# Three shared-expert products done as seven products of halves, and two routed sums moved ahead of the conditional block

## The chip, the cores and the metric

The kernel runs on one core of one Trainium2 chip. The core has a matrix engine (TensorE, PE in the profile), a vector engine (VectorE, DVE), a scalar engine (ScalarE, ACT), a general engine (GpSimd, POOL) and a queue engine (SyncE, SP). Each executes its own instructions strictly in the order in which they were written and waits on semaphores for the others. 16 DMA engines move data between the chip's large memory (HBM) and the on-chip memory; transfers are issued by SP (plain copies) and POOL (row gathers by a list of indices). TensorE writes into eight PSUM banks of 128 x 512 f32. The metric is the device time of one execution in microseconds (us).

## The reference

One transformer-like block on x of shape (B, T, H) = (4, 512, 512), all in float32. A conditioned layer norm, a time mix and a channel mix with its own residuals come first; then a second conditioned layer norm gives the rows h for a mixture of experts:

```
h = _layernorm(x) * (1 + cb) + sb
sh_mid = gelu(einsum('th,ehd->ted', xt, Wsh_up))            # 2 shared experts, H 512 -> D 256, every row
shared_out = einsum('ted,edh->th', sh_mid, Wsh_down)        # D 256 -> H 512, summed over both experts
probs = softmax(xt @ W_router); top_v, top_i = top_k(probs, 2)
rt_mid = gelu(einsum('th,ehd->ted', xt, Wrt_up))            # 16 routed experts, two of them for each row
routed_out = einsum('ted,edh->th', rt_mid * gate, Wrt_down)
x = x + gb * (shared_out + routed_out)
```

The reference computes all 16 routed experts; the kernel computes only the two that a row has picked.

## The kernel before, in words

**Stages.** Time mix for the batches 0 to 3, then channel mix (whose large products are already done as seven products of half-size blocks instead of eight), then the experts. The times at which they lie in the profile: the experts begin at about 720 us and end with the span.

**Who decides the order.** Nothing is scheduled by a planner: the instruction order on each engine is the order of the Python code. Where two stages are to overlap, one is a generator that is advanced by the other: `weave(main, back, plan)` runs `main` to its next `yield` and then advances `back` by the next number of the plan (1 when the plan has run out). For batch 1 the time mix is woven with `time_front(2)`, the layer norms of batch 2, by the plan (2, 1, 2, 1, 2) (L1376). A step of `time_front` holds a tile's `statistics` (L194 to L199), `nm` (L212), the normed rows `xn_ln` (ACT, L219) or the transposes `ps_t_ln` (PE, L226).

**Buffers.** 64 row tiles of 128 x 512 f32 (`row_tile`, tag "t", used in rotation: a new tile waits for all users of the tile that is given up), 8 weight tiles of 1 MB (`wpool`: two stay with the shared experts `wsh_0` and `wsh_1`, six hold the weights of routed experts), and 8 PSUM banks in two tags ("ps" and "acc") of four each.

**Routed experts: slots.** The rows are sorted by expert into slots of 128 rows. 41 slots (N_FIRST) always run; up to 6 more run under `tc.If(n_used > N_FIRST)` (L1426), which this data does not take. `slots_by(b)` = 23, 31, 39, 47 says after which slot all rows of batch b are done. The loop is a pipeline of five steps over the slots. Iteration s issues: `turn(s)` (four transposes of the gathered rows, L1222, copied by DVE, L1224), `up(s-1)` (L1230, GELU on ACT L1232), `turn_mid(s-2)` (L1238, copied by DVE, L1240), `down(s-3)` (L1246, copied by ACT, L1248), `keep(s-4)` (store of 256 KB to y_d by SP, L1252) and then `fetch(s+3)`: a gather of 128 rows by POOL (L1207) and two loads of 512 KB of weights by SP (L1201, L1202). No weight can be loaded more than three slots ahead, and a load waits until `down` has freed its tile.

**Shared experts.** Per batch, `shared_up` makes four groups of PE work (per expert and half of D: four k-steps of 128 x 512, L1152) with a GELU on ACT each (L1158), and `shared_down` four more (one per tile of 128 rows, four steps of 128 x 512, L1166), which `scaled_onto` multiplies by gb (L1177) and adds to x (L1178) on DVE. `shared_up` of batches 0 and 1 and `shared_down` of batch 0 run before the slots (L1398). Then `groups`, `shared_down(1)` and `shared_up(2)`, is advanced by one group after every other slot: s = 22, 24, 26, 28 and s = 30, 32, 34, 36. The four groups of `shared_up(3)` (`last_ups`) follow in the iterations 41 to 44.

**Routed results.** `gather(b, t)` (POOL, L1276) brings two rows of y_d per token for tile t: for batch 0 at s = 28 to 31, batch 1 at s = 36 to 39, batch 2 at s = 43 and 44 (two tiles each), batch 3 after the conditional block. `routed` (ACT L1292 multiplies one by its gate; DVE L1293 adds the other; then `scaled_onto`) does batches 0 and 1 two iterations after their gather, `store_out` (SP, L1305) one later.

**Tail.** After the conditional block, for the eight tiles of batches 2 and 3: four matmuls of `shared_down` (L1166), then `routed_and` on DVE, which adds both routed rows to the PSUM tile (L1300, L1301) and then calls `scaled_onto`: four DVE operations per tile. The last tile's routed part is done apart (L1293), and its shared part in two halves of 256 columns (L1444) that lie in one PSUM bank, each with a multiply (L1452), an add (L1453) and a store.

## Time and profile before

| | |
|---|---|
| device time, median of 3 runs | 1027.38 us (1027.22 to 1028.17) |
| the profiled execution, its own time | 1028.34 us |
| its span, first to last instruction | 1026.5 us (1.84 us lie around the span) |
| TensorE busy | 1003.0 us, 98%, granted clock 0.997 |
| VectorE, ScalarE, GpSimd busy | 616.8, 319.8, 342.3 us |
| moved by DMA | 182.83 MB |

How to read it: busy times of the engines overlap, so they are not added up; what counts is the chain in which each piece waits for the one before. A matmul's shown duration runs from its issue to its modelled end; the next one starts before that end, so the distance from start to start is what a matmul costs in a dense row. A float32 matmul of the code appears as two records. "DMA share" in a table by stretches is the mean busy share of the 16 DMA engines (it can be a little above 1 by its reckoning), beside the GB/s that they moved.

### The profile page before, as it was taken

What the parts mean: (1) busy time and instruction counts of PE and PEld (TensorE: products, weight loads), DVE (VectorE), ACT (ScalarE), POOL (GpSimd) and SP (SyncE); (2) the same over time, 40 slices, a digit from 0 to 9 for tenths busy, and PEclk for the clock granted to TensorE, in tenths of its full rate; (3) what the DMA queues carried; (4) which work ended last, traced back from release to release, by engine and by line L of the source; (5) the groups of instructions that cost most, each with busy time, mean ns of one, the idle gap of its engine ahead of it and who ended that gap; (6) DMA issues with size and microseconds to landing.
All of it is one profiled execution on the core that took longest, in us unless ns stands there. A gap on an engine that the chain in (4) does not pass through costs nothing. (4 is left out here: it accounts for less than half of the span.)

```text
span 1026.5 us, 11651 instructions
## 1 busy us (share of the span) xinstructions
PE 1003.0 (98%) x3930; PEld 685.8 (67%) x3930; DVE 616.8 (60%) x1181; ACT 319.8 (31%) x530; POOL 342.3 (33%) x324
## 2 busy tenths in 40 slices
PE   7999999999999999999999999999998999999997
PEld 2444444444688888888888888888646676666643
DVE  5787887797665736848757587428654222233426
ACT  1765645653222305320262203220021222122310
POOL 2463563514354105620266006520104221232160
PEclk9999999999999999999999999999999999999999
DMA  9600401352069562365226534650536999899762
GB/s 328 247 0 2 125 19 42 103 192 86 1 225 349 178 233 83 121 232 178 88 76 215 195 133 175 240 180 1 185 123 187 365 382 383 270 321 316 266 194 83
DMA packets 96765, 182.83 MB, mean 178 GB/s; under 512 B 7528, under 2 KB 50280, under 8 KB 92608
## 3 DMA queue, kind: packets, MB, share of 16 engines
q1 hardware_dynamic: 90864, 162.92, 45.6%
q0 software_dynamic: 5840, 19.14, 5.8%
q8 instruction: 32, 0.52, 0.2%
q14 instruction: 29, 0.24, 0.1%
HBM read 149.75 MB, written 32.29 MB: 177 GB/s over the span
## 5 line engine op out<-in xcount | busy, mean ns | idle before, releaser
L199 POOL TENSOR_TENSOR rstd_ln<-rstd_ln,minus_half 128x1 f32<-128x1 f32 x64 | 42.9, 672 | 199.5 <-DVE rstd_ln L198 182.5
L782 PE MATMUL ps_y<-wval,a 128*128 128x256 f32 x384 | 86.0, 380 | 0.0
L1207 POOL DMA_INDIRECT xg<-h_d,token x41 | 39.5, 963 | 127.9 <-PE ps_xt L1222 44.8
L782 PEld LDWEIGHTS ps_y<-wval,a 128*128 128x128 f32 x384 | 72.3, 190 | 12.0 <-issue 2.5
L1230 PE MATMUL ps_up<-wrt,xt 128*128 128x256 f32 x328 | 78.0, 381 | 0.3 <-ACT act L1232 0.2
L1246 PE MATMUL ps_down<-wrt,at 128*128 128x512 f32 x164 | 77.2, 593 | 0.0
L1230 PEld LDWEIGHTS ps_up<-wrt,xt 128*128 128x128 f32 x328 | 59.1, 190 | 8.0 <-DVE xt L1224 1.0
L1224 DVE COPY xt<-ps_xt 128x512 f32<-128x512 f32 x41 | 28.2, 689 | 56.2 <-PE ps_xt L1222 42.1
L711 PE MATMUL ps_ky<-T,keys_hi 128*128 128x256 f32 x256 | 60.6, 380 | 0.0
L711 PE MATMUL ps_kx<-mix_ln,keys_lo 128*128 128x256 f32 x256 | 60.5, 379 | 0.0
L357 PE MATMUL ps_o<-wo,av 128*128 128x512 f32 x128 | 57.4, 597 | 2.4 <-DVE x L427 1.2
L352 PE MATMUL ps_r<-mix_ln,wr 128*128 128x512 f32 x128 | 57.6, 593 | 0.8 <-issue 0.8
L782 PE MATMUL ps_z<-wval,a 128*128 128x256 f32 x256 | 57.9, 380 | 0.0
L352 PE MATMUL ps_v<-mix_ln,wv 128*128 128x512 f32 x128 | 57.5, 592 | 0.0
L782 PE MATMUL ps_x<-wval,a 128*128 128x256 f32 x256 | 57.2, 379 | 0.0
L1152 PE MATMUL ps_up_sh<-h,wsh 128*128 128x512 f32 x128 | 57.2, 593 | 0.0
L394 DVE RECIPROCAL p<-p 128x512 f32<-128x512 f32 x16 | 53.6, 3353 | 0.6
L1166 PE MATMUL ps_down_sh<-wsh,mid 128*128 128x512 f32 x120 | 53.1, 595 | 0.3 <-PEq L1426 0.3
L711 PEld LDWEIGHTS ps_kx<-mix_ln,keys_lo 128*128 128x128 f32 x256 | 48.5, 190 | 6.9 <-issue 0.5
L711 PEld LDWEIGHTS ps_ky<-T,keys_hi 128*128 128x128 f32 x256 | 48.3, 190 | 6.8 <-DVE ku L749 0.4
L782 PEld LDWEIGHTS ps_z<-wval,a 128*128 128x128 f32 x256 | 48.1, 190 | 6.8 <-issue 0.6
L782 PEld LDWEIGHTS ps_x<-wval,a 128*128 128x128 f32 x256 | 48.2, 190 | 6.3
(260 smaller groups left out, 1845.3 us busy)
## 6 DMA issues: line engine op xcount, KB each, us to landing
wrt<-in_rt_up_dram SPq DMA_DIRECT2D x41, 512.0 KB
wrt<-in_rt_down_dram SPq DMA_DIRECT2D x41, 512.0 KB
wval<-sums_d SPq DMA_DIRECT2D x16, 1024.0 KB
wval<-in_wval_t_dram SPq DMA_DIRECT2D x12, 1024.0 KB
keys_lo<-keys_d SPq DMA_DIRECT2D x12, 1024.0 KB
y_d<-y SPq DMA_DIRECT2D x41, 256.0 KB
keys_hi<-keys_d SPq DMA_DIRECT2D x12, 768.0 KB
mod<-mod_d SPq DMA_DIRECT2D x22, 256.0 KB
```

Source lines behind the costliest of these rows:

```text
L199: nc.gpsimd.tensor_tensor(rstd, rstd, minus_half, ALU.pow)
L352: nc.tensor.matmul(ps, w[:, k, m * P : (m + 1) * P], acts[k], start=(k == 0), stop=(k == NK - 1))
L357: nc.tensor.matmul(ps, acts[k][:, t * P : (t + 1) * P], w[:, k, :], start=(k == 0), stop=(k == NK - 1))
L394: nc.vector.reciprocal(p, p)
L711: nc.tensor.matmul(ps[:, c * HT : (c + 1) * HT], w[:, k, c * P : (c + 1) * P], acts[k], start=(fresh and c == 0 and k == 0), stop=(c == 1 ...
L782: nc.tensor.matmul(ps[:, j * HT : (j + 1) * HT], acts[p][:, c, j * P : (j + 1) * P], w[:, i, :], start=(fresh and i == 0 and j == 0), stop ...
L1152: nc.tensor.matmul(ps, wu[:, k, m * P : (m + 1) * P], h3s[b][k], start=(k == 0), stop=(k == NK - 1))
L1166: nc.tensor.matmul(ps, mids[b][j][:, t * P : (t + 1) * P], shared[j // ND][1][:, j % ND, :], start=(j == 0), stop=(j == len(mids[b]) - 1),)
L1207: nc.gpsimd.indirect_dma_start(out=xg, out_offset=None, in_=h3_d, in_offset=bass.IndirectOffsetOnAxis(ap=token[:, s : s + 1], axis=0),)
L1224: nc.vector.tensor_copy(xt.rearrange("p k t -> p (k t)"), ps)
L1230: nc.tensor.matmul(ps[:, :D], xt[:, k, :], wu[:, k, :], start=(k == 0), stop=(k == NK - 1))
L1246: nc.tensor.matmul(ps, at[:, j, :], wd[:, j, :], start=(j == 0), stop=(j == ND - 1))
```

## The change

Three of the eight shared products are done as seven products of half-size blocks (`shared_down(1)`, `shared_up(2)` and `shared_up(3)`); the products of batch 0, `shared_up(1)` and the `shared_down` of batches 2 and 3 stay direct.

- `shared_sums` (new) makes eight sums or differences of weight blocks on DVE (128 x 512 each), in the slot loop at s = 3; one of them overwrites a block of `wsh_1` in place.
- `shared_down_terms` and `shared_up_terms` (new) make the sums of the other operand on DVE, one slot ahead of the group: at s = 23, 28 and 40.
- `seven` (new) issues the seven products (28 matmuls of 256 columns), with the additions that combine them on DVE and three copies by ACT. The groups are no longer spread: `shared_down(1)` lies in one piece after slot iteration 24, `shared_up(2)` after 29, both with a short rest of DVE work an iteration later; of `shared_up(3)` four products are issued at s = 41 and three after the loop.
- `shared_up` now writes its GELU results in pieces of 128 x 256 (two ACT instructions in place of one), since blocks of halves are needed.
- `routed(2, 0)` and `routed(2, 1)` are issued before the rest of `shared_up(3)` and the conditional block, wholly on DVE (the gate's multiply too).
- In the tail `routed_and` is gone. The routed sums are issued one tile ahead (`routed`: ACT, DVE), and `scaled_onto` takes the PSUM tile alone. The two halves of the last tile lie in PSUM banks of their own.
- The weave plan for batch 1's time mix is (2, 2, 1, 2) in place of (2, 1, 2, 1, 2).

The diff, cut to its core:

```diff
     def shared_up(b, halves=False):
-        mids[b] = []
-        for wu, _ in shared:
+        mids[b] = [[row_tile(f"mid_{b}_{t}_{f}", (P, ND, HT)) for f in range(E_SH)] for t in range(2)]
+        for f, (wu, _) in enumerate(shared):
             for m in range(ND):
-                ps = bank(f"ps_up_sh_{b}_{len(mids[b])}")
+                ps = bank(f"ps_up_sh_{b}_{f}_{m}")
                 for k in range(NK):
                     nc.tensor.matmul(
                         ps, wu[:, k, m * P : (m + 1) * P], h3s[b][k], start=(k == 0), stop=(k == NK - 1)
                     )
                     if halves and k % 2:
                         yield
-                act = row_tile(f"mid_{b}_{len(mids[b])}", (P, T))
-                nc.scalar.activation(act, ps, AF.Gelu)
-                mids[b].append(act)
+                for t in range(2):
+                    nc.scalar.activation(mids[b][t][f][:, m, :], ps[:, t * HT : (t + 1) * HT], AF.Gelu)
...
+    def shared_sums():
+        for i, j in blocks:
+            ups[f"A{i + 1}{j + 1}"] = shared[i][0][:, j * ND : (j + 1) * ND, :]
+            downs[f"B{i + 1}{j + 1}"] = shared[i][1][:, :, j * HT : (j + 1) * HT]
+        def add(where, name, one, other, op):
+            where[name] = row_tile(f"sh_{name}", (P, ND, HT))
+            nc.vector.tensor_tensor(where[name], where[one], where[other], op)
+        add(ups, "S3", "A11", "A21", ALU.subtract)
+        ups["S1"] = ups["A21"]
+        nc.vector.tensor_add(ups["S1"], ups["A21"], ups["A22"])
+        add(ups, "S2", "S1", "A11", ALU.subtract)
+        add(ups, "S4", "A12", "S2", ALU.subtract)
+        add(downs, "T1", "B12", "B11", ALU.subtract)
+        add(downs, "T3", "B22", "B12", ALU.subtract)
+        add(downs, "T2", "B22", "T1", ALU.subtract)
+        add(downs, "T4", "B21", "T2", ALU.subtract)
...
+    def seven(name, product, A, Bs, use, parts=False):
+        X = bank(f"{name}_x")
+        product(X, A["A11"], Bs["B11"], True)
+        c1 = copied(f"{name}_c1", X)
+        Y = bank(f"{name}_y", "acc")
+        product(Y, A["S2"], Bs["T2"], True)
+        u = row_tile(f"{name}_u")
+        nc.vector.tensor_add(u, c1, Y)
+        Z = bank(f"{name}_z", "acc")
+        product(Z, A["S1"], Bs["T1"], True)
+        c5 = copied(f"{name}_c5", Z)
+        nc.vector.tensor_add(c5, c5, c1)
+        product(X, A["A12"], Bs["B21"], False)
+        use(0, 0, X)
+        if parts:
+            yield
+        product(Y, A["S3"], Bs["T3"], False)
+        nc.vector.tensor_add(c5, c5, Y)
+        use(1, 1, c5)
+        product(Z, A["S4"], Bs["B22"], False)
+        nc.vector.tensor_add(u, u, Z)
+        use(0, 1, u)
+        product(Y, A["A22"], Bs["T4"], False)
+        yield
+        nc.vector.tensor_add(c1, c1, Y)
+        use(1, 0, c1)
+        yield
+    def halves_product(stationary, moving):
+        def product(ps, a, b, fresh):
+            for c in range(2):
+                for k in range(2):
+                    nc.tensor.matmul(
+                        ps[:, c * HT : (c + 1) * HT],
+                        stationary(a, k, c),
+                        moving(b, k),
+                        start=(fresh and c == 0 and k == 0),
+                        stop=(c == 1 and k == 1),
+                        skip_group_check=True,
+                    )
+        return product
+    acts_of = {}
+    def shared_up_terms(b):
+        acts = {f"B{i + 1}{j + 1}": [h3s[b][2 * i + k][:, j * HT : (j + 1) * HT] for k in range(2)] for i, j in blocks}
+        for name, one, other in (("T1", "B12", "B11"), ("T3", "B22", "B12"), ("T2", "B22", "T1"), ("T4", "B21", "T2")):
+            t = row_tile(f"h3_{name}_{b}", (P, 2, HT))
+            acts[name] = [t[:, k, :] for k in range(2)]
+            for k in range(2):
+                nc.vector.tensor_sub(acts[name][k], acts[one][k], acts[other][k])
+        acts_of[b] = acts
+    def shared_up_seven(b, parts=False):
+        acts = acts_of.pop(b)
+        mids[b] = [[None] * 2 for _ in range(2)]
+        def use(f, t, v):
+            act = row_tile(f"mid_{b}_{t}_{f}")
+            nc.scalar.activation(act, v, AF.Gelu)
+            mids[b][t][f] = act.rearrange("p (c t) -> p c t", c=2)
+        product = halves_product(lambda w, k, c: w[:, k, c * P : (c + 1) * P], lambda a, k: a[k])
+        yield from seven(f"up_sh_{b}", product, ups, acts, use, parts)
...
+    def shared_down_seven(b):
+        A = acts_of.pop(b)
+        def use(i, j, v):
+            at = slice(j * HT, (j + 1) * HT)
+            add = row_tile(f"add_sh_{b}_{i}_{j}", (P, 2, HT))
+            row = gbs[b][:, None, at].broadcast_to([P, 2, HT])
+            nc.vector.tensor_tensor(add, v.rearrange("p (t o) -> p t o", t=2), row, ALU.mult)
+            for t in range(2):
+                xt = x1s[b][2 * i + t][:, at]
+                nc.vector.tensor_add(xt, xt, add[:, t, :])
+        product = halves_product(lambda a, k, c: a[:, k, c * P : (c + 1) * P], lambda w, k: w[:, k, :])
+        yield from seven(f"down_sh_{b}", product, A, downs, use)
...
-    def routed(b, t):
+    def routed(b, t, engine=None):
         g0, g1 = gates_of(b, t)
         y0, y1 = got.pop((b, t))
-        nc.scalar.activation(y1, y1, AF.Copy, scale=g1)
+        if engine is nc.vector:
+            nc.vector.tensor_scalar(y1, y1, g1, None, ALU.mult)
+        else:
+            nc.scalar.activation(y1, y1, AF.Copy, scale=g1)
         nc.vector.scalar_tensor_tensor(y0, y0, g0, y1, ALU.mult, ALU.add)
-        scaled_onto(b, t, y0)
-    def routed_and(b, t, ps):
-        g0, g1 = gates_of(b, t)
-        y0, y1 = got.pop((b, t))
-        nc.vector.scalar_tensor_tensor(y0, y0, g0, ps, ALU.mult, ALU.add)
-        nc.vector.scalar_tensor_tensor(y0, y1, g1, y0, ALU.mult, ALU.add)
         scaled_onto(b, t, y0)
     def store_out(b, t):
...
-        weave(time_mix(b), back, (2, 1, 2, 1, 2) if b == 1 else ())
+        weave(time_mix(b), back, (2, 2, 1, 2) if b == 1 else ())
...
-    groups = chained(lambda: shared_down(1), lambda: shared_up(2))
-    last_ups = shared_up(B - 1)
+    down_1 = slots_by(0) + 1, lambda: shared_down_terms(1), chained(lambda: shared_down_seven(1))
+    up_2 = slots_by(0) + 6, lambda: shared_up_terms(2), chained(lambda: shared_up_seven(2))
+    up_3 = N_FIRST, lambda: shared_up_terms(3), chained(lambda: shared_up_seven(3, True))
     at = [slots_by(b) + 5 for b in range(B - 1)]
     for s in slots(0, N_FIRST, ready):
-        if s >= slots_by(0) - 1 and (s - slots_by(0)) % 2:
-            next(groups, None)
+        if s == AHEAD:
+            shared_sums()
+        for lag, (first, terms, group) in ((-1, down_1), (-1, up_2), (-1, up_3), (0, down_1), (0, up_2), (1, down_1), (1, up_2)):
+            if s == first + lag:
+                if lag < 0:
+                    terms()
+                else:
+                    next(group)
...
-        if s >= N_FIRST:
-            next(last_ups)
-    drain(groups)
-    drain(last_ups)
+        if s == N_FIRST:
+            next(up_3[2])
+    for t in range(NT // 2):
+        routed(B - 2, t, nc.vector)
+    for group in (down_1, up_2, up_3):
+        drain(group[2])
     n_used = nc.values_load(used[0:1, 0:1], min_val=0, max_val=N_SLOT)
     with tc.If(n_used > N_FIRST):
         drain(slots(N_FIRST, N_SLOT))
     for t in range(NT):
         gather(B - 1, t)
-    for b in (B - 2, B - 1):
-        for t in range(NT):
-            ps = down_bank(b, t)
-            if b == B - 1 and t == NT - 1:
-                break
-            down_products(b, t, ps, range(4))
-            if b == B - 1 and t == NT - 2:
-                routed(b, NT - 1)
-            routed_and(b, t, ps)
-            store_out(b, t)
+    rest = [(B - 2, t) for t in range(NT // 2, NT)] + [(B - 1, t) for t in range(NT)]
+    routed(*rest.pop(0))
+    for n in range(2 * NT - 1):
+        b, t = B - 2 + n // NT, n % NT
+        ps = down_bank(b, t)
+        down_products(b, t, ps, range(4))
+        scaled_onto(b, t, ps)
+        store_out(b, t)
+        if rest:
+            routed(*rest.pop(0))
     last = x1s[B - 1][NT - 1]
     for at in (slice(0, HT), slice(HT, H)):
+        ps = bank(f"ps_last_{at.start}", "acc")
         for j in range(4):
             nc.tensor.matmul(
-                ps[:, at],
-                mids[B - 1][j][:, (NT - 1) * P :],
+                ps[:, :HT],
+                mid_of(B - 1, j, NT - 1),
                 shared[j // ND][1][:, j % ND, at],
                 start=(j == 0),
                 stop=(j == 3),
             )
-        add = row_tile(f"add_last_{at.start}")
-        nc.vector.tensor_mul(add[:, at], ps[:, at], gbs[B - 1][:, at])
-        nc.vector.tensor_add(last[:, at], last[:, at], add[:, at])
+        add = row_tile(f"add_last_{at.start}", (P, HT))
+        nc.vector.tensor_mul(add, ps[:, :HT], gbs[B - 1][:, at])
+        nc.vector.tensor_add(last[:, at], last[:, at], add)
         nc.sync.dma_start(out[B - 1, (NT - 1) * P :, at], last[:, at])
```

More of the change, by code (lines that the diff above doesn't have):

```diff
@@ L1162, in shared_up, with mid_of @@
         h3s[b] = None
+    def mid_of(b, j, t):
+        return mids[b][t // 2][j // ND][:, j % ND, (t % 2) * P : (t % 2 + 1) * P]
+    blocks = [(i, j) for i in range(2) for j in range(2)]
+    ups, downs = {}, {}
+    def shared_sums():
[14 more added lines that the diff above has]
+        add(downs, "T4", "B21", "T2", ALU.subtract)
@@ new lines, in copied @@
+    def copied(name, ps):
+        t = row_tile(name)
+        nc.scalar.activation(t, ps, AF.Copy)
+        return t
+    def seven(name, product, A, Bs, use, parts=False):
[25 more added lines that the diff above has]
+        yield
@@ new lines, in shared_up_seven @@
+    def shared_up_seven(b, parts=False):
[7 more added lines that the diff above has]
+        yield from seven(f"up_sh_{b}", product, ups, acts, use, parts)
+        h3s[b] = None
@@ new lines, in shared_down_terms @@
+    def shared_down_terms(b):
+        A = {f"A{t + 1}{f + 1}": mids[b][t][f] for t, f in blocks}
+        for name, one, other, op in (
+            ("S1", "A21", "A22", ALU.add),
+            ("S2", "S1", "A11", ALU.subtract),
+            ("S3", "A11", "A21", ALU.subtract),
+            ("S4", "A12", "S2", ALU.subtract),
+        ):
+            A[name] = row_tile(f"mid_{name}_{b}", (P, 2, HT))
+            nc.vector.tensor_tensor(A[name], A[one], A[other], op)
+        acts_of[b] = A
+    def shared_down_seven(b):
[10 more added lines that the diff above has]
+        yield from seven(f"down_sh_{b}", product, A, downs, use)
@@ L1167, in down_products @@
                 ps,
-                mids[b][j][:, t * P : (t + 1) * P],
+                mid_of(b, j, t),
                 shared[j // ND][1][:, j % ND, :],
                 start=(j == 0),
-                stop=(j == len(mids[b]) - 1),
+                stop=(j == E_SH * ND - 1),
             )
```

## The prediction

> **What bounds the kernel now.** I read the page first, then the table by stretches, then the order of time on TensorE, then the chain of waits at the end.
>
> ```profile
> span 1026.5 us, 11651 instructions
> ...
> PE 1003.0 (98%) x3930; PEld 685.8 (67%) x3930; DVE 616.8 (60%) x1181; ACT 319.8 (31%) x530; POOL 342.3 (33%) x324
> ```
>
> TensorE is the bound: only 23.5 us of the span are not its work, and the list of its waits names 1.8 us of them in time mix and 3.3 us in the tail. So a change is worth what it takes from TensorE's stream, less the waits that it puts in. Inside the slots the stretches say something else as well:
>
> ```profile
> 800.00:810.00 10.00, 10.00 (x46) 6.89 (x45) 2.66 (x5) 2.56 (x5) 2.08 (x3) 1.00 1.06 379
> ...
> 900.00:910.00 10.00, 10.00 (x38) 5.97 (x37) 3.36 (x6) 1.96 (x4) 5.67 (x6) 1.00 0.98 332
> ...
> 920.00:930.00 10.00, 10.00 (x40) 6.31 (x39) 4.52 (x9) 3.39 (x6) 2.02 (x2) 1.00 0.94 297
> ...
> 940.00:950.00 10.00, 10.00 (x40) 6.34 (x39) 2.23 (x4) 2.41 (x5) 5.67 (x6) 1.00 0.95 316
> ```
>
> The columns after each engine's busy time are the clock, DMA share and GB/s. In plain slots (first row) TensorE is full and the DMA engines are full too, 1.06. A plain iteration moves 1.573 MB (two weights of 512 KB, a gather and a store of 256 KB) and takes 4.10 us: 384 GB/s. There DMA has nothing to spare. Only the groups of shared work between the slots give it time.
>
> ```profile
> 878.02 3.60 PE L1166 MATMUL ps_down_sh<-wsh,mid 128*128 128x512 f32 x8
> 881.45 0.60 PE L1222 MATMUL ps_xt<-ident,xg 128*128 128x128 f32 x4
> 881.89 1.89 PE L1230 MATMUL ps_up<-wrt,xt 128*128 128x256 f32 x8
> 883.62 0.38 PE L1238 MATMUL ps_at<-ident,act 128*128 128x128 f32 x2
> ```
>
> From start to start, eight records of 512 columns take 881.45 - 878.02 = 3.43 us, eight of 256 columns 1.73 us. The "mean ns" of the groups (593 and 380) overlap and would mislead.
>
> **The change, part by part.**
>
> *Seven products.* A direct shared product is 4 groups x 8 records of 512 columns: 4 x 3.43 = 13.72 us. Seven products are 28 matmuls, 56 records of 256: 7 x 1.73 = 12.11 us, 1.6 us less. Down 1 and up 2 give -3.2 if nothing waits inside. The additions (128x512 on DVE, 0.69 to 0.75 each) and ACT copies (0.60) stand beside: a bank is written again 3.46 us after its first product, and in one place 1.73 us after, behind one DVE add of 0.72 and at most 1.5 us of `use` begun a product earlier. It is tight but fits; a wait would cost up to 0.8 a group: -3.2, ends -3.2 and -1.6. Their terms (four 128x512 or eight 128x256 adds, 3 us) lie on a DVE that is busy 2.7 to 4.5 of 10 us. The doubled GELUs of batches 0 and 1 (two 128x256 of 0.4 for one of 0.60, every 3.43 us on an ACT at 31%) cost nothing; were that cover gone, 16 x 0.2 = 3.2.
>
> *Weight sums at s = 3.* Eight DVE operations go in behind at_1's copy and ahead of xt_4's.
>
> ```profile
> 788.61 0.41 DVE L1240 COPY at<-ps_at 128x256 f32<-128x256 f32 x1
> 788.94 0.68 DVE L1224 COPY xt<-ps_xt 128x512 f32<-128x512 f32 x1
> ...
> 792.96 1.24 PE L1230 MATMUL ps_up<-wrt,xt 128*128 128x256 f32 x5
> ```
>
> at_1 is done at 789.02; eight adds, start to start 0.72 as L1177's, end at 794.8; xt_4's copy (0.69) at 795.5. The up products that read it began at 792.96, so TensorE waits 2.5 us. at_2's copy, next in the queue, ends at 795.9, before its `down` at 797.4: no second wait. Ends: 2.0 (if an add took 0.66), and 4.2, if the pause also slows the matmuls as the tail's does (1.7, below). Idle times of 1.65 us (786) and 1.81 us (117) were not followed by slow matmuls, one of 3.27 us was; 2.5 is nearer the short ones, so 2.5. The Trainium skill, "TensorE: Matmul & The Clock Gate", Part 1, has the clock halved only after an idle window of about 3.4 us; that adds 0 here (and 1.7 in the other case), though the trace's 3.27 us already was enough.
>
> *Groups taken out of s = 30 to 40.* Before, four groups of up 2 lie there; now eleven plain iterations follow each other, 11 x 4.10 = 45.1 us. They carry 11 x 1.573 = 17.30 MB and, before slot 40's weights, two of batch 0's tiles gathered (1.05), its four stores (1.05) and about half of batch 1's gathers (1.05): 20.45 MB. At 384 GB/s that is 53.3 us. What TensorE's use may lag: a weight is issued at the end of iteration s and first needed in iteration s+4, 12.5 us later; less its slot's own 4.1 us and 2.5 us of latency (batch 2's last gather: issued 984.7, landed 987.3), about 6. 53.3 - 45.1 - 6 = 2.2 us of waiting near s = 38 to 41. Ends: 0 (before, with groups, no wait appears there but 0.8 for rows), and from the mixed rows: at full share 1.06 they would give 332 x 1.06/0.98 = 359, 335 and 353, mean 349 GB/s; 20.45 MB take 58.6 us, a wait of 7.5. I take 2.2, by the full rows, since the mixed ones had moments with nothing issued. SP's and POOL's orders change little otherwise: no transfer passes another on its queue. What speaks against this part in the Trainium skill is "DMA: Bandwidth & Descriptors", Where 436 GB/s comes from: about 358 GB/s bind a core's HBM traffic; then the wait would be 57.1 - 51.1 = 6.0 us and the sum 3.8 worse, but the plain slots ran at 379 to 385.
>
> *Up 3 and the tail.*
>
> ```profile
> 989.98 20.85 PE ps_down_sh L1166 x48
> ...
> 1018.86 0.34 DVE add_last L1452
> 1019.21 0.04 issue
> 1019.25 3.45 PE ps_down_sh L1444 x8
> 1022.72 0.44 DVE add_last L1452
> 1023.18 0.42 DVE x L1453
> ```
>
> The second half of the last tile waits 3.27 us for the multiply that reads the first half from the same bank, and then takes 3.43 in place of 1.73 us. With a bank each, both go: -5.0, and 0.2 of small gaps. Up 3 as seven: -1.6. Against it: the routed sums of batch 2's tiles 0 and 1 (four operations, 2.9 us each) stand on DVE ahead of up 3's last additions. Their gathers landed 11.4 and 13.9 us after up(40) began (968.36), so DVE ends them at about 17.2. The product that waits for the add behind them is due at 17.8, the add takes 0.7: +0.1, and with gathers a little later +0.8, which I take; ends 0 and 2.5 (one gather pair later). In the tail DVE has per tile a multiply and an add from PSUM and a routed sum of three, 5 operations, 3.65 us against 3.43 of TensorE; it has one routed sum less than tiles ahead and none for the last two, falls 1.1 us behind by the fifth and has caught up by the last. ACT's multiply (0.71) fits. Part: -6.0, ends -4.0 and -6.8.
>
> *The weave plan.* Batch 2's tiles 2 and 3 get their statistics a step earlier.
>
> ```profile
> 112.49 3.35 DVE L394 RECIPROCAL p<-p 128x512 f32<-128x512 f32 x1
> ...
> 115.76 0.10 DVE L212 SCALAR_TENSOR_TENSOR nm_ln<-mv_ln,rstd_ln 128x1 f32<-128x1 f32 x1
> ```
>
> nm of tile 3 stands behind the reciprocal, ACT's xn_ln behind nm, and TensorE's transposes wait 1.81 us at 116.77. Now nm precedes the reciprocal: -1.8. Late next is the reciprocal's own chain, 1.2 us (one tile's statistics); its reader has 2.6 us to spare. Ends 0 and -1.8.
>
> **Sum.** -3.2 + 2.5 + 2.2 - 6.0 - 1.8 = -6.3. The profiled execution's 1028.34 us (1026.5 of span, 1.84 around it) would become 1022.0. It lies 0.96 above the median of the three runs; against that median of 1027.38 I get 1021.1, which is my number. 0.2%, about what a measurement of this kernel can tell from no change, is 2.05 us: faster is below 1025.3, slower above 1029.4.
>
> **Rivals.**
>
> *Both new waits are hidden.* DMA keeps its slack (0 for 2.2), the tail gets its best (-6.8): -3.2 + 2.0 - 6.8 - 1.8 = -9.8, 1017.6. For it: DMA had 9 to 11 us of slack between landing and use there before. Against: the groups that gave it are gone.
>
> *DMA is the bound from s = 30 to 41, at a lower rate than the plain slots'.* At 349 GB/s the wait is 7.5 and the sum -1.0: 1026.4, no change. It decides the sign at 10.6 us of waiting: 20.45 MB in 61.7 us, 331 GB/s. At 306, the mean of the rows 920 and 940, it is 66.8 us, a wait of 15.7, +7.2: 1034.6, slower. For it: gathers of rows and writes are mixed with the loads there, and no mixed row but one exceeds 332. Against: TensorE was never held by weights in those rows, and 910 to 920 gave 370.
>
> *The products save nothing.* By the means, seven cost 56 x 380 = 21.3 against 32 x 593 = 19.0 us, +2.3 each, 11.7 us from my sum: +5.4, 1032.8. Against: channel mix runs such products at 1.73 us per eight without a gap.
>
> *DVE sets the tail's end.* 7 x 3.65 = 25.6 against 24.0 and the two waits in it: the part gives -4.0, 1023.1.
>
> **How the numbers follow.** My forecast, with what lies within 3 us of it (the DVE-bound tail too): 0.52. All hidden: 0.14. DMA bound at about 349: 0.12. DMA bound below 331: 0.15. Products without gain: 0.04; the rest 0.03. The range leaves out the two slow cases and little below: from all best (-3.2 + 2.0 + 0 - 6.8 - 1.8 = -9.8, and 1.6 below for what I can't see: 1016) to the end of the 349 case and 1.6 above, 1028. Faster: 0.52 + 0.14 + a part of the 349 case, 0.07: 0.73. Same: 0.05 and the rest, 0.09. Slower: 0.18.
>
> **What would show it.** L226's longest wait for xn_ln at 117 us falls below 0.5. L1230 has one wait of about 2.5 us at 793 for xt. The groups after s = 24 and 29 take 12.1 us without a gap. Between 950 and 965 a wait of TensorE for `wrt` or `xg` of about 2 us in all, and a DMA share above 1 from s = 33 on. No wait at the last halves, both 1.73 us. I am wrong if the waits of s = 30 to 41 pass 5 us, if slow matmuls follow the pause at 793, or if TensorE waits inside `seven`.

## The result, and the profile after

The changed kernel takes 1024.11 us (median of 9 runs, 1022.03 to 1025.98) beside 1027.65 us of the kernel before on the same chip: a ratio of 0.996, 95% interval 0.9947 to 0.9974. It is faster, by 3.5 us where 6.3 were forecast. The profiled execution took 1025.98 us with a span of 1024.3; against the profiled execution of before that is only 2.4 us less, and the readings below account for these two. The nine runs of the changed kernel differ with the granted clock: the three with 0.997 or 0.998 took 1022.03 to 1022.17 us, the six with 0.994 to 0.996, the profiled one among them as the longest, 1023.97 to 1025.98.

The page of the changed kernel begins:

```profile
span 1024.3 us, 11869 instructions
...
PE 1000.3 (98%) x4002; PEld 699.6 (68%) x4002; DVE 646.7 (63%) x1237; ACT 327.0 (32%) x549; POOL 343.8 (34%) x324
```

TensorE is busy 2.7 us less, though three products of 1.6 us each were saved and 1.7 us of slow matmuls at the end are gone: part of its time is spent at a lower clock. Its list of waits (total, times, longest) names what is new:

```profile
PE ps_t_ln L226 <- ACT xn_ln L219: 5.0, 5, 1.5
PE up_sh_y L1233 <- DVE up_sh_c L1216: 2.5, 1, 2.5
...
PE ps_up L1363 <- DVE xt L1357: 1.9, 2, 1.6
PE ps_o L357 <- DVE x L427: 1.7, 3, 1.0
PE ps_down_sh L1299 <- DVEq L1564: 1.1, 1, 1.1
```

The wait of 3.3 us at the last halves is gone, and three others stand in its place: 2.5 us inside up 3, 1.6 us at the slots' end, 1.1 us at the conditional block (L1564). The order of time on TensorE shows where:

```profile
874.07 1.89 PE L1233 MATMUL down_sh_x<-wsh,mid 128*128 128x256 f32 x8
...
884.43 1.89 PE L1233 MATMUL down_sh_y<-sh_T,mid 128*128 128x256 f32 x8
886.16 0.60 PE L1355 MATMUL ps_xt<-ident,xg 128*128 128x128 f32 x4
...
956.50 1.89 PE L1363 MATMUL ps_up<-wrt,xt 128*128 128x256 f32 x8
...
962.34 1.99 PE L1363 MATMUL ps_up<-wrt,xt 128*128 128x256 f32 x8 [1.57 <-DVE xt L1357]
...
966.41 1.97 PE L1363 MATMUL ps_up<-wrt,xt 128*128 128x256 f32 x8
...
982.44 1.89 PE L1233 MATMUL up_sh_z<-h,sh_S 128*128 128x256 f32 x8
986.85 2.55 PE L1233 MATMUL up_sh_y<-h_T,wsh 128*128 128x256 f32 x8 [2.52 <-DVE up_sh_c L1216]
990.46 26.51 PE L1299 MATMUL ps_down_sh<-wsh,mid 128*128 128x512 f32 x56 [1.07 <-DVEq L1564]
1016.81 3.62 PE L1583 MATMUL ps_last<-wsh,mid 128*128 128x256 f32 x16
```

These are the lines of the kernel before for slots 38 and 40 and for the tail:

```profile
960.40 1.89 PE L1230 MATMUL ps_up<-wrt,xt 128*128 128x256 f32 x8
...
968.36 1.99 PE L1230 MATMUL ps_up<-wrt,xt 128*128 128x256 f32 x8
...
989.98 24.27 PE L1166 MATMUL ps_down_sh<-wsh,mid 128*128 128x512 f32 x56 [0.30 <-PEq L1426]
1014.09 1.89 PE L1444 MATMUL ps_down_sh<-wsh,mid 128*128 128x256 f32 x8
1019.25 3.43 PE L1444 MATMUL ps_down_sh<-wsh,mid 128*128 128x256 f32 x8 [3.27 <-DVE add_last L1452]
```

Down 1's seven products take 886.16 - 874.07 = 12.09 us without a gap, and the last halves about 3.5 us together. But the seven tiles of the tail take 1016.81 - 990.46 = 26.35 us, where the kernel before took 24.1 and the kernel without the conditional block, below, 24.04. The stretches (last columns: clock, DMA share, GB/s) say why:

```profile
985.00:990.00 5.00, 2.55 (x8) 1.61 (x8) 2.92 (x5) 1.23 (x2) 0.68 (x2) 0.81 0.45 143
990.00:995.00 5.00, 4.54 (x6) 1.99 (x7) 2.26 (x4) 2.12 (x4) 3.88 (x4) 0.50 0.50 139
995.00:1000.00 5.00, 5.00 (x13) 2.20 (x12) 3.49 (x6) 1.29 (x2) 3.98 (x4) 1.00 0.72 218
```

The granted clock is halved from 988.15 to 994.97: it falls 1.3 us after the pause of 2.52 us, while up 3's last product runs, and is already down when the pause of 1.07 us begins at 989.4. Set against each other, the starts of the same TensorE work in the two profiles, with what the prediction's terms add up to at that point:

| TensorE starts | before | after | difference | predicted |
|---|---|---|---|---|
| k products of batch 2 | 116.93 | 114.80 | -2.13 (-0.38 of it from the first 9 us) | -1.8 |
| o products, batch 2 | 214.25 | 213.55 | -0.70 | -1.8 |
| transposes after channel mix (L923) | 741.32 | 741.24 | -0.08 | -1.8 |
| up(4) | 792.96 | 792.34 | -0.62 | +0.7 |
| up(38) | 960.40 | 956.50 | -3.90 | -2.5 |
| up(40) | 968.36 | 966.41 | -1.95 | -0.3 |
| first matmul of the tail | 989.98 | 990.46 | +0.48 | -1.1 |
| end of VectorE's last addition | 1023.60 | 1021.34 | -2.26 | -6.3 |

At up(40) the changed kernel is 1.6 us ahead of the forecast, by errors of both signs. The forecast was missed behind it: 2.4 us were lost between up(40) and the tail where 0.8 should have been won, and the tail won 2.7 in place of 5.2, because 2.3 went into slow matmuls. Another 0.7 went into up 3's last product, which took 2.55 us in place of 1.89.

### The profile page after: what moved, and what is told of

Same layout as the page of the kernel before. It is cut to its first block, busy times and chain, and to the rows that moved or that the text cites. A ratio compares the mean times of both kernels' runs of the same rounds, so it can differ in the third digit from the quotient of the medians.

```text
span 1024.3 us, 11869 instructions
## 1 busy us (share of the span) xinstructions
PE 1000.3 (98%) x4002; PEld 699.6 (68%) x4002; DVE 646.7 (63%) x1237; ACT 327.0 (32%) x549; POOL 343.8 (34%) x324
## 5 line engine op out<-in xcount | busy, mean ns | idle before, releaser
L1409 POOL DMA_INDIRECT y<-y_d,pos_i x32 | 32.0, 999 | 58.7 <-DMA y_d<-y 35.1
L219 ACT ACTIVATE xn_ln<-x,nm_ln,rstd_ln 128x512 f32<-128x512 f32 x32 | 25.3, 810 | 77.5 <-DVE nm_ln L212 77.5
```

The costliest lines, as they stand in the source:

```text
L1409: nc.gpsimd.indirect_dma_start(out=y, out_offset=None, in_=y_d[: slots_by(b) * P, :], in_offset=bass.IndirectOffsetOnAxis(ap=pos_i[:, c, n ...
```

## The experiments

They ran in three sets, each beside the kernel before on its chip: 1026.36 us in the first (four kernels), 1028.3 and 1028.24 us in the others. Ratios are to these.

### Routed sums behind up 3

```diff
-    for t in range(NT // 2):
-        routed(B - 2, t, nc.vector)
     for group in (down_1, up_2, up_3):
         drain(group[2])
+    for t in range(NT // 2):
+        routed(B - 2, t, nc.vector)
```

> The changed kernel with one edit: the two routed sums of batch 2 stand behind the rest of up 3 on VectorE, not ahead of it (still before the conditional block). Theory 1, the two sums hold up the last product of up 3 and the pause halves TensorE's clock: the wait of 2.52 us at up_sh_y disappears (under 0.5), the clock stays full through the tail, its 56 matmuls of the shared down take 24.0 in place of 26.5 us, and TensorE comes to the last halves 5 to 6 us earlier than in the changed kernel's profile; the end follows if VectorE keeps up, 1019 to 1021 us. Rival, VectorE sets the tail's end: it has the same work left (about 3.65 us per tile and 5.4 us for the two sums), so the end moves by less than 2 us and TensorE waits for banks or VectorE ends alone: 1022 to 1024 us.

Measured: 1026.93 us, 1.0003 (0.9994 to 1.0012), no faster than the kernel before. The wait inside up 3 went, as expected, but TensorE then stood still for longer. TensorE, then VectorE's last routed addition, in order of time:

```profile
984.03 1.89 PE L1233 MATMUL up_sh_y<-h_T,wsh 128*128 128x256 f32 x8
992.26 27.05 PE L1299 MATMUL ps_down_sh<-wsh,mid 128*128 128x512 f32 x56 [6.34 <-DVEq L1564]
...
991.23 0.69 DVE L1311 TENSOR_TENSOR x<-x,add 128x512 f32<-128x512 f32 x1
```

The first tile of the tail needs nothing from the routed sums. It starts 0.34 us after VectorE has left them behind, and the wait is named by VectorE's branch at the conditional block. Both theories had missed this: VectorE does not set the end through its load in the tail, it holds TensorE at the block. A new theory: the PSUM bank of the first tile has its last reader, in program order, inside the block (VectorE's copy `at` of slot 46), and that reader counts as done only when VectorE itself has passed the block, taken or not. The program built from this kernel agrees: the first tile's matmul waits until VectorE's count of finished instructions stands at 1213, which is the copy `at` of slot 46; where the block is not taken, VectorE adds the block's 12 counts in one step, behind a wait for count 1201, its last routed addition.

### The conditional block left out

The kernel of the last experiment without `tc.If`:

```diff
-    n_used = nc.values_load(used[0:1, 0:1], min_val=0, max_val=N_SLOT)
-    with tc.If(n_used > N_FIRST):
-        drain(slots(N_FIRST, N_SLOT))
```

> The kernel with the routed sums behind up 3 (1.0003 of the kernel before), and the conditional block with its six optional slots left out; for these inputs it is not taken, so nothing that is computed is missing. Theory: TensorE's 6.3 us ahead of the tail are a wait for VectorE to pass the block, since the bank of the first tile has its last reader in program order inside it. Without the block the first tile waits for a bank's true last reader: the wait falls to under 1.5 us, the clock stays full, and the end comes 5 to 7 us earlier: 0.993 to 0.996 of the kernel before. Rival, TensorE needs a result of VectorE's queue there (the last addition of up 3 or a routed sum): the wait stays over 3 us and the time within 2 us.

Measured: 1023.95 us, 0.9951 (0.9935 to 0.9967). TensorE goes on without a gap and with the full clock:

```profile
989.42 1.89 PE L1233 MATMUL up_sh_y<-h_T,wsh 128*128 128x256 f32 x8
991.14 24.20 PE L1299 MATMUL ps_down_sh<-wsh,mid 128*128 128x512 f32 x56
```

989.42 + 1.73 = 991.15: no wait at all, with the routed sums in the same place on VectorE, where they end only at 997.3. The block is what ties TensorE to VectorE there. (At 966.28 this profile has a wait of 3.33 us with slow matmuls after it, one of the late signals of the last section.) (In other data, where more than 41 slots are used, this kernel would leave rows out; it is an experiment and not a version.)

### Another bank for the first tile

```diff
-        ps = down_bank(b, t)
+        ps = bank(f"ps_down_sh_{b}_{t}", "ps" if n == 0 else "acc")
```

This too is the kernel with the sums behind up 3.

> The kernel with the routed sums behind up 3 (1.0003 of the kernel before), with one edit: the first tile of the tail lies in a bank of the other tag, whose last user inside the conditional block is read by ScalarE and not by VectorE. Theory: TensorE's 6.34 us ahead of the tail are a wait for VectorE to pass the conditional block, because the bank of the first tile was last read, in program order, by VectorE inside that block. With the other bank the first tile waits for ScalarE alone, which is through at about 987.5: the first tile starts 4 to 5 us earlier (about 987.7) and the second waits at its own bank to about 992.3, so that the tail ends 3.4 us earlier (one tile); with less idle time the halved clock may go as well, 2 us more: -3.4 to -5.5, 0.995 to 0.997. Rival, TensorE waits for the branch value or for VectorE's results: no change, 1.000.

Measured: 1032.46 us, 1.0043 (1.0026 to 1.0059). The wait did not change:

```profile
PE ps_down_sh L1299 <- DVEq L1564: 6.4, 1, 6.4
```

The edit missed its aim: in the program the bank of the other tag, too, is read by VectorE inside the block (the copy `xt` of slot 43), and the first tile waits for that copy beside ScalarE. It tells nothing against the theory and nothing for it. On this chip the kernel also waited 1.86 us at up(39) with slow matmuls after it, which is about the rest of its loss.

### Three products direct again, dense

Down 1, up 2 and up 3 direct in the same places, no sums:

```diff
-        if s == AHEAD:
-            shared_sums()
-    down_1 = slots_by(0) + 1, lambda: shared_down_terms(1), chained(lambda: shared_down_seven(1))
-    up_2 = slots_by(0) + 6, lambda: shared_up_terms(2), chained(lambda: shared_up_seven(2))
-    up_3 = N_FIRST, lambda: shared_up_terms(3), chained(lambda: shared_up_seven(3, True))
+    down_1 = slots_by(0) + 1, lambda: None, chained(lambda: shared_down(1))
+    up_2 = slots_by(0) + 6, lambda: None, chained(lambda: shared_up(2))
+    up_3 = N_FIRST, lambda: None, chained(lambda: shared_up(3))
...
-                if lag < 0:
-                    terms()
-                else:
-                    next(group)
+                if lag == 0:
+                    drain(group)
...
             next(up_3[2])
+            next(up_3[2])
```

> The changed kernel with the three shared products done directly again, in the same places (dense after s = 24, 29, 41 and after the loop), without the sums of weights and of operands; the rest of the change (weave plan, routed sums ahead, new tail) stays. Theory: down 1 and up 2 cost 2 x 1.6 = 3.2 us more, up 3 1.6 more; the wait at s = 3 (0.4) goes, and so does the wait of the last product (2.5), since direct groups wait for no additions, with the halved clock behind it (2.9): net -1.0, 1022 to 1024 us. Rival, the products save nothing by themselves: down 1 takes 12.1 us either way and the result is 3 us or more below the changed kernel. If the halved clock comes without the wait too, the result is above it, 1026.

> All three products direct, dense, with the new tail and plan, as run before (0.9953 of the kernel before): the same again, 0.994 to 0.997, so that the two other kernels of this set are compared with it on one chip.

Measured: 1021.43 us in the first set, 0.9953 (0.994 to 0.9967); 1027.72 us in the third, 0.999 (0.9979 to 1.0). In the first set's profile the tail is what the prediction had drawn:

```profile
980.83 7.03 PE L1153 MATMUL ps_up_sh<-h,wsh 128*128 128x512 f32 x16
988.16 24.27 PE L1299 MATMUL ps_down_sh<-wsh,mid 128*128 128x512 f32 x56 [0.30 <-PEq L1561]
1012.27 3.62 PE L1580 MATMUL ps_last<-wsh,mid 128*128 128x256 f32 x16
```

Direct groups leave VectorE nothing to add, it passes the block early, TensorE waits 0.3 us, and the tail takes 24.1 us. Without any of the seven products the kernel is not slower than the change: on that chip it is the fastest of its set. In the third set the same kernel gained next to nothing; its TensorE waited 1.73 us at 788, 2.17 us at 965 and 1.34 us at 969, none of which the first set's profile has. The last section comes back to that.

### Up 3 alone direct

```diff
-    up_3 = N_FIRST, lambda: shared_up_terms(3), chained(lambda: shared_up_seven(3, True))
+    up_3 = N_FIRST, lambda: None, chained(lambda: shared_up(3))
...
             next(up_3[2])
+            next(up_3[2])
```

Its up 3 reads the block of `wsh_1` that the sums have overwritten, so the shared part of batch 3 is computed from another weight; instructions and sizes are those of the direct product. The kernel of the section after the next shares this.

> The changed kernel with up 3 alone done directly (two groups at s = 41, two after the loop); down 1 and up 2 stay seven products with their sums. Theory: direct groups leave no additions on VectorE behind the routed sums, so VectorE reaches the conditional block before TensorE, TensorE waits 0.3 us there and its clock stays full: 990.46 becomes about 987 and the tail 24.0 us; against the kernel with all three direct (0.9953 of the kernel before) 3.2 us less for the two products, 0.4 more for the sums at s = 3 and 1.7 more for weights that land late at s = 41: -1.1, so about 1020.3 beside 1026.4 of before, 0.994. Rival, the conditional block is not it and the seven products are what costs the time in the slots: no gain over all three direct, 1021.4 or more.

Measured: 1024.34 us, 0.996 (0.9946 to 0.9973). The wait at the block is 0.3 us and the tail 991.00 to 1015.11, 24.1 us, so the block's part of the theory held. The gain over direct products did not show, but the chip was another one, so the comparison was made again side by side:

### Sums one per slot, beside direct products dense and spread

Up 3 direct; the eight sums one per slot from s = 6, S1 in a tile of its own (so nothing is overwritten). The sums' function yields after each, and the loop advances it:

```diff
+    the_sums = shared_sums()
...
-        if s == AHEAD:
-            shared_sums()
+        if s >= AHEAD + 3:
+            next(the_sums, None)
```

> The changed kernel with up 3 direct (down 1 and up 2 stay seven products), the sums of weights one per slot from s = 6 on, in place of eight at s = 3, and none of them in place. Theory: one sum of 0.7 us per slot is hidden, so the two products keep 3.2 us less the 1.7 that late weights take at s = 41: 1.5 us less than the kernel with all three products direct, which runs beside it. Rival, DMA sets the time from s = 30 to 41 and takes all of it: the same time as with direct products, within 0.5 us.

The third kernel has all products direct, and their groups where the kernel before has them:

```diff
+    groups = chained(lambda: shared_down(1), lambda: shared_up(2))
...
+        if s >= slots_by(0) - 1 and (s - slots_by(0)) % 2:
+            next(groups, None)
...
-        if s == N_FIRST:
-            next(up_3[2])
-            next(up_3[2])
+        if s >= N_FIRST:
+            next(up_3[2])
```

> All three products direct, and their groups spread over the slots as in the kernel before (after s = 22, 24, 26, 28; 30, 32, 34, 36; 41 to 44); the new tail and the routed sums ahead of the block stay. Theory: what the change gains is the tail; where the direct groups stand makes no difference, since TensorE waits for no weights in either: within 0.5 us of the dense form beside it. Rival, dense groups cost DMA time that the spread ones use, or the spread ones leave less for the slots at 39 and 40: 1 to 2 us apart.

Measured in one set: seven products with spread sums 1023.89 us, 0.9955 (0.9942 to 0.9968); direct and spread 1024.1 us, 0.9956 (0.9942 to 0.997); direct and dense 1027.72 us. The theory that the place of direct groups makes no difference fell on this chip: dense they were 3.6 us slower, with the waits named above. Two products as seven, dense, worth 3.2 us of TensorE's work, are 3.8 us faster than direct products in the same dense places, but bring nothing over direct groups that are spread. On this chip the late signals of the last section weigh on each of the three differently, so what the seven products are worth by themselves is not settled. TensorE's order of time near the end of the slots shows where their lead goes; first with the seven products:

```profile
956.62 1.89 PE L1370 MATMUL ps_up<-wrt,xt 128*128 128x256 f32 x8
960.00 0.44 PE L1378 MATMUL ps_at<-ident,act 128*128 128x128 f32 x2 [1.49 <-issue]
960.76 3.46 PE L1386 MATMUL ps_down<-wrt,at 128*128 128x512 f32 x4 [0.32 <-DVE at L1380]
...
964.71 1.89 PE L1370 MATMUL ps_up<-wrt,xt 128*128 128x256 f32 x8
...
968.38 1.97 PE L1370 MATMUL ps_up<-wrt,xt 128*128 128x256 f32 x8
```

and then direct and spread, the same three `up` steps (slots 38, 39, 40):

```profile
961.32 1.89 PE L1363 MATMUL ps_up<-wrt,xt 128*128 128x256 f32 x8
...
965.43 1.89 PE L1363 MATMUL ps_up<-wrt,xt 128*128 128x256 f32 x8
...
969.29 1.99 PE L1363 MATMUL ps_up<-wrt,xt 128*128 128x256 f32 x8
```

At up(38) the products have put TensorE 4.7 us ahead, at up(39) 0.7. Here the loss is a late signal with halved clock behind it. On the first set's chip, where no signal was late, the pair of kernels "sums behind up 3" and "direct, dense" gives the same picture by another cause: up(38) at 956.57 against 958.58, 2.0 us ahead, and up(40) at 966.28 against 966.54, 0.3 us. There the list names VectorE's `h_T`, but xt of slot 40 was done at 964.47, and what came last in the trace is slot 40's weights: their last packet landed at 966.14. Whoever comes early waits for them. The changed kernel's own trace agrees: the last recorded packet of these weights landed at 966.28, and its up(40) starts at 966.41, so its wait of 1.57 us at up(39) would have been spent at up(40) otherwise.

### Up 2's products after s = 36

```diff
-    up_2 = slots_by(0) + 6, lambda: shared_up_terms(2), chained(lambda: shared_up_seven(2))
+    up_2 = slots_by(0) + 13, lambda: shared_up_terms(2), chained(lambda: shared_up_seven(2))
```

> The kernel with up 3 alone direct, and up 2's seven products after s = 36 in place of s = 29. Theory: the wait for weights at s = 41 is lack of DMA time between s = 30 and 41; the 12.1 us of products put there give DMA 4.6 MB more time, and the wait of 1.7 us at up(40) goes: 1.7 us less than with the products after s = 29. Rival, the late landing comes from batch 1's gathers at s = 36 to 39 alone, which stay: the wait stays, no difference.

Measured: 1026.88 us, 0.9989 (0.9979 to 0.9999), 2.5 us slower than with the products after s = 29, beside which it ran. At its own place the theory held: up(39) and up(40) follow each other at 967.55 and 971.41, without a wait. But a new wait appears where the products had been:

```profile
903.22 1.89 PE L1363 MATMUL ps_up<-wrt,xt 128*128 128x256 f32 x8
...
913.36 0.44 PE L1371 MATMUL ps_at<-ident,act 128*128 128x128 f32 x2 [4.14 <-issue]
...
912.92 0.38 ACT L1365 ACTIVATE act<-ps_up 128x256 f32<-128x256 f32 x1 [9.34 <-remote]
```

ScalarE's GELU began at 912.92, though the `up` that it reads had been issued at 903.22 and lasted 1.9 us: 7.8 us late. Batch 0's gathers are under way there; with the dense products after s = 29 TensorE has work there that can hide such a delay.

### Sums at s = 10

```diff
-        if s == AHEAD:
+        if s == 10:
             shared_sums()
```

> The changed kernel with the eight sums of weights at s = 10 in place of s = 3. The prediction's step priced them at 2.5 us of waiting of TensorE, and the changed kernel showed 0.5, at a place where TensorE itself was late. Theory: in a settled iteration the price is the full one, one wait of up(11) for xt of 2.3 to 2.7 us at about 820 us, with no slow matmuls after it. Rival, VectorE's queue has room for most of it: under 1 us.

Measured once: 1029.84 us beside 1028.3. The expected wait of 2.3 to 2.7 us does not come; the rival, under 1 us, holds:

```profile
819.45 0.68 DVE L1180 TENSOR_TENSOR sh_S<-wsh,wsh 128x512 f32<-128x512 f32 x1
...
824.83 0.68 DVE L1357 COPY xt<-ps_xt 128x512 f32<-128x512 f32 x1
...
825.56 1.99 PE L1363 MATMUL ps_up<-wrt,xt 128*128 128x256 f32 x8 [0.31 <-DVE xt L1357]
```

Eight sums take 5.4 us, and the `up` was due at 825.1: 0.5 us late. From a settled iteration's `at` copy to the next but one `up` there are 5.6 us and not the 3.9 that the prediction had read at s = 3. The rest of this kernel's loss lies elsewhere: waits of 1.7 us at 788 and 3.25 us at up(39), each with 3.4 us at half clock behind it.

### The weave plan alone

```diff
-        weave(time_mix(b), back, (2, 1, 2, 1, 2) if b == 1 else ())
+        weave(time_mix(b), back, (2, 2, 1, 2) if b == 1 else ())
```

> The kernel before with the new weave plan for batch 1's time mix and nothing else. The prediction's step: -1.8 us, 1025.8 beside 1027.6. Theory now, from the changed kernel's trace: the wait at 117 us goes, but ScalarE and VectorE, which were full there, do not come earlier, so TensorE waits for them at 208 to 214 us and at 739 us, and 0 to -0.4 us are left: 1027.2 to 1027.6.

Measured: 1026.78 us, 1.0003 (0.9994 to 1.0012): nothing. Its TensorE has the three lines that the changed kernel has too:

```profile
116.22 3.60 PE L352 MATMUL ps_k<-mix_ln,wk 128*128 128x512 f32 x8
...
209.76 0.33 PE L226 MATMUL ps_t_ln<-ident,xn_ln 128*128 128x128 f32 x1 [0.38 <-ACT xn_ln L219]
...
214.97 1.55 PE L357 MATMUL ps_o<-wo,av 128*128 128x512 f32 x3 [1.01 <-DVE x L427]
```

Against the run of before's code in the same set (the kernel of the next experiment, which differs from it only in the tail) the transposes at 116 us come 2.12 us earlier and the products at 215 only 0.69, of which 0.38 is an earlier start of the whole sequence in this profile: 1.7 us won and 0.3 left. ScalarE is busy 9.3 and 9.9 of 10 us from 115 to 135 in the kernel before, and its chain with VectorE's reciprocals would then set when the next batches' operands are there; that is argued from these shares and not shown by a run.

### Two banks for the last halves alone

```diff
     for at in (slice(0, HT), slice(HT, H)):
+        ps = bank(f"ps_last_{at.start}", "acc")
         for j in range(4):
```

on the kernel before.

> The kernel before with a PSUM bank of its own for each half of the last tile and nothing else. Theory: the wait of 3.27 us and the slow second half both go, 3.3 + 1.7 = 5.0 us less at most; VectorE's last additions then come 3 us earlier, at the end of its own queue: it is at 1019.2 when the first half's multiply is issued, so the end cannot come before 1018.8 + 4 x 0.43 = 1020.5 us of the span, and I expect -3.0 us, 1024.6. Rival: the slow clock comes anyway, since TensorE idles after the first tiles in the same way: -1.5 us.

Measured: 1023.6 us, 0.9969 (0.9957 to 0.9981), 3.2 us by the ratio. The halves take 3.5 us from 1013.11, and VectorE, which has four operations per tile in one piece, ends later:

```profile
1013.11 3.62 PE L1445 MATMUL ps_last<-wsh,mid 128*128 128x256 f32 x16
...
1018.59 0.42 DVE L1453 TENSOR_TENSOR add_last<-ps_last,mod 128x256 f32<-128x256 f32 x1
1019.04 0.42 DVE L1454 TENSOR_TENSOR x<-x,add_last 128x256 f32<-128x256 f32 x1
```

By the ratios, taken in different sets, this one line is worth three quarters of what the whole change gains (0.0031 of 0.0040). No version tried beats the change beyond the intervals; direct, spread products with the new tail (0.9956) are as fast and much simpler.

## Why the prediction was right or wrong

The sign and the range were right; 6.3 us were forecast and 3.5 came. One of the prediction's own signs of being wrong did come true: TensorE waited 2.5 us inside `seven`, in up 3. Step by step:

- **Seven products, -3.2.** Right inside the groups: 12.09 us each, no wait, and the slots came 3.3 us earlier between up(4) and up(38). Not shown as a gain of the kernel: direct products spread over the slots end at the same time as two products as seven (0.9956 against 0.9955), and the all-direct, dense kernel was the fastest of its set on one chip and 3.6 to 3.8 us slower than those two on the other.
- **Weight sums, +2.5.** Too high: 0.5 at s = 3 and 0.5 at s = 10. The step took the distance from at_1's copy to up(4) in an iteration in which VectorE was running late; in a settled one it is 5.6 us. A single early occurrence was read where settled ones stood right behind it in the trace.
- **Slots 30 to 41, +2.2.** Mechanism right, and the size as well: 1.95 us were lost between up(38) and up(40) in the changed kernel, 1.7 in the first set's kernel, and slot 40's weights, landed at 966.28 and 966.14, ended it in both. That the size came out so near is in part luck: the sum took 2.5 us of latency from a gather "issued 984.7, landed 987.3", but that gather's last recorded packet in the trace of before came at 989.26, 4.5 us after its issue; with that the sum would have given 4.2. What I did not draw from it: if the weights set the time at up(40), most of what is saved before it is lost there as well (of 2.0 us ahead of the direct kernel 0.3 were left), so the two terms are one. The rival "DMA is the bound" was the better description, with the plain slots' rate.
- **Up 3, +0.8 (0 to 2.5).** The wait was 2.52, at the end of the range: the two gathers had landed 13.6 and 17.1 us after up(40) began (VectorE starts on them at 980.05 and 983.47), not 11.4 and 13.9. Those two figures were issue times plus the same 2.5 us; in the trace of before the last recorded packets of these gathers came at 981.64 and 983.83, 13.3 and 15.5 us after up(40). Outside every bound lay what followed: the conditional block, at which the additions of up 3 hold TensorE 0.8 us longer than before, and the halved clock behind the pause (2.3 us in the tail, 0.7 in the product). "Each engine passes the block by itself" was an unspoken assumption of that step, and the experiments without the block and with the sums behind up 3 show that it is false for the first tile of the tail.
- **Tail, -5.2.** Right: no wait at the last halves, about 3.5 us for both, VectorE 0.9 us behind TensorE at the end. It was the only part with a lasting gain.
- **Weave plan, -1.8.** Right at its place (1.75 us) and worth nothing: 0.9 and 0.5 us were taken back between 207 and 214 us, and 0.6 more at 738 to 741. The step asked only for the reciprocal's next reader, where 2.6 us were to spare; it did not follow ScalarE's and VectorE's work, which had not become less, to its next meeting with TensorE.

Of the Trainium skill's two rules, "TensorE: Matmul & The Clock Gate", Part 1, was named for pricing the clock after a pause of 2.5 us at nothing: an idle window of about 3.4 us is what it asks for. Here a pause of 2.52 us was enough, and 6.8 us ran at half clock; the measurement decides. "DMA: Bandwidth & Descriptors", Where 436 GB/s comes from, with its 358 GB/s, would by an estimate from that figure have made the wait 6.0 us; the 1.7 to 2 us measured are on the side of the row.

## What to carry to other kernels

Follow a saving to the next point at which another resource hands over: work saved ahead of loads that run at full rate, or ahead of a full ScalarE, is given back there. Before a conditional block, count every instruction that any engine still has to execute: here a buffer whose last reader stands inside the block was released only when that reader's engine had passed it, so a few additions on VectorE became 6.3 us of TensorE. Read the price of a queued burst in a settled iteration, and try the one-line part of a large change by itself first.

## What the runs showed that was not expected

- **Pauses below 3.4 us halve the clock, depending on where they fall.** 1.65 and 1.81 us in the kernel before did not; 2.52 us in the changed kernel did, for 6.8 us, and in the kernel with spread sums 1.49 with 0.32 us did, for 3.4 us (the `down` of 3.46 us above, twice its usual time). The stretches at half clock last 3.41 us or two or three times that, and they start on a grid of the same step: at 25.59 and 988.15 in the changed kernel, 282 steps apart, at 26.36 and 1019.64 in the kernel before, 291 steps. What the traces bear out is the idle time within one step. It was 2.11 us in the step that ends at 988.15, 3.02 in the one that ends at 1019.64 and 1.81 in the one of the spread sums, all followed by half clock; the two short pauses of the kernel before left 1.65 and 1.66 us. Past the first 5 us of the fourteen profiles, every step at full clock with more than 2.1 us idle was followed by half clock and none with less than 1.8; between 1.81 and 1.94 us both occur. So a pause of 2.5 us is free or costs 1.7 us or more by where the grid cuts it, which the code does not set. At the start of the kernel the half clock lasted 3.4 us in the profiles of the two kernels and 10.2 us in most others.
- **Signals came late during gathers, in most profiles.** In the profiles of the two kernels and of the second and third sets, instructions that wait for TensorE, on an engine that is free, start up to 3.9 us (kernel before), 3.1 us (changed kernel) and 7.8 us (up 2's products after s = 36) after the recorded end of the matmul, while GpSimd issues row gathers one behind the other (about 780, 905 and 955 us). In the four profiles of the first set no signal of TensorE came more than 0.5 us late. In the changed kernel the 1.57 us at up(39) belong here: TensorE's transposes of slot 39 were recorded at 956.07, and VectorE, free at 960.78, copied them at 961.59. What delays the signals stays open. How much it can weigh is seen in the direct, dense kernel, 0.9953 on one chip and 0.999 on the other: the waits at 788, 965 and 969 us, 5.2 us in all, are in the slower profile alone. That they are the whole difference is not shown.
